# The rows that stand apart: W_q times (W_k transposed times the rows), two heads at once, in place of the folded weights times the rows

## The chip, the cores and the metric

The kernel runs on one core of a Trainium2 chip. The metric is the device time of one execution in microseconds (us), the median of several runs; lower is better. Engines are named as in the profile: PE (TensorE matmuls), PEld (its weight loads), DVE (VectorE), ACT (ScalarE), POOL (GpSimd) and SP (the queue that issues nearly all DMAs). All arithmetic that matters here is float32, and one float32 matmul of the program stands as two records in the trace; a transpose on PE stands as one.

## The reference, cut to what matters

The model has two layers. Each begins with a cross attention in which 64 latent rows per batch element (16 batch elements, 128 numbers wide) attend, in 16 heads of 64, over the 1601 rows of a context and over themselves:

```
xn, ln_lat = layer_norm(x, g1, b1), layer_norm(latents, g2, b2)
q  = ln_lat @ Wq
kv = concatenate([xn, ln_lat], axis=1) @ Wkv
k, v = split(kv, 2, axis=-1)
weight = softmax(einsum('bhld,bhnd->bhln', q * scale, k * scale))     # scale**2 = 1/8
out = einsum('bhln,bhnd->bhld', weight, v)
return out.transpose(0, 2, 1, 3).reshape(b, l, heads * dim_head) @ Wout
```

After the attention come, in layer 0, a state-space scan and a mixture of experts, and in layer 1 another scan and a feed-forward part. They are woven between the attention's tiles and are not touched by the change.

## The kernel before

**Folded weights.** The score of a latent row with a context row in head h is ln_lat · (Wq_h Wk_hᵀ / 8) · xnᵀ. The kernel folds the two weights of each head into one 128x128 matrix once per layer (`fold_qk`, which runs `fold`, matmuls L344, evictions L349 and L351), kept in `wqk`. `queries` (L455) multiplies the latents by it, and `scores` (L662) multiplies the result with the context rows as they are. `fold_vo` folds the value and the output weights in the same way into `wvo` (tiles `WvT`, also L344).

**Tiling.** A group is one batch element and eight heads, so there are 64 groups. A group's scores are made in 13 tiles of 128 context rows by 512 columns (eight heads times 64 latents). 13 tiles hold 1600 context rows and the 64 latent rows. One context row of the 1601 is left over for each batch element: these 16 rows "stand apart".

**The rows that stand apart.** `apart(lay)` prepares them once per layer. It normalises the 16 rows (L370 to L382), writes them to DRAM (`xed`, L383), transposes them (`xet` L386, copied into `xeT`, 128x16), and then makes `ge`, which holds for each batch element and head the 128-vector (Wq_h Wk_hᵀ / 8) · row. Before the change it does so from `wqk`, four heads at a time and four times: PE transposes four 128x128 matrices into a PSUM tile (`wkq`, L394), ACT copies it to SBUF (`wkq0s`, L396), PE multiplies each by `xeT` (L399, 16 columns), and DVE copies the result into `ge` (L400). `apart_scores` (L409, L414) later multiplies the latents of two batch elements by `ge`; `maximum` needs its result.

**What sets the order.** The program is recorded in steps `n`, one per score tile. In each step the loop in `run` resumes the generators whose turn has come (`yield HOP3` asks to be resumed three steps later, a plain number only ends the step's share), and `behind` ties what they emit to the last score tile of each engine, so that each engine executes in an order fixed beforehand. DMAs issued from SP are placed more freely. All engines execute their own list strictly in order: an instruction that waits holds up all behind it on its engine.

**Buffers that the change touches.** `tp` gives PSUM tiles from a pool of three banks, shared by the transposes, `kt`, `q`, `WqT`, `WvT`, `wkq`, `ge`, `se` and others; a new tile waits until an older one in its bank has been read. The score tiles have three banks of their own. In SBUF the tag `raw` has three buffers of 2 KB per partition: they hold `xw`, the four `wkq0s`, and the raw weights of layer 1. The tag `st2` has twelve buffers: the scores of a group take six, and the raw weights of layer 0 (`raw0`, loaded first of all) use four of them until they are given back.

**Who stands behind `apart(0)`.** While it runs, the kernel is still filling its pipeline. On DVE the statistics of the second batch element's context (L594, L595) lie between its instructions; they end in `crstd` (L598). POOL then takes its power of minus one half (L135), makes `coff` (L600, L601), ACT normalises eight tiles with it (L606), SP stores the normalised context (`xh`, L632), and behind that store on SP stand the loads of the raw weights for `fold_vo(0)`.

Of the kernel before, what the change touches and what calls it, by code (L numbers as in the profile page):

```python
# [32 lines left out]
F32 = mybir.dt.float32  # L33
# [9 lines left out]
P = 128  # L43
NB, L, D = 16, 64, 128
# [6 lines left out]
H, DH = 16, 64  # L51
# [13 lines left out]
HOP1, HOP, HOP3, HOP4 = (1,), (2,), (3,), (4,)  # L65
# [14 lines left out]
class Kernel:  # L80
# [273 lines left out]
    def fold_qk(self, lay):  # L354
        self.wqk = self.at.tile([P, H, D], F32, tag="wqk", name=f"wqk{lay}")
        yield from self.fold(lay, self.wqk, "WqT", "WkT", 0.125)
        self.raw0 = None

    def fold_vo(self, lay):
        self.wvo = self.at.tile([P, H, D], F32, tag="wvo", name=f"wvo{lay}")  # L360
# [1 line left out]
    def apart(self, lay):  # L362

        nc = self.nc
        w1 = self.vecs_of(lay)[0]
        xe = self.xe
        if lay == 0:
            mean, rstd, v = (self.sm([NB, 1], f"e{x}") for x in ("mean", "rstd", "var"))
            scr = self.at.tile([NB, D], F32, tag="raw", name="escr", bufs=3)
            nc.vector.tensor_reduce(mean, xe, AX.X, ALU.add)  # L370
            nc.vector.tensor_scalar_mul(mean, mean, 1.0 / D)
            nc.vector.tensor_scalar(xe, xe, mean, None, ALU.subtract)
            nc.scalar.activation(scr, xe, AF.Square)
            yield HOP1
            nc.vector.tensor_reduce(v, scr, AX.X, ALU.add)
            nc.vector.tensor_scalar(v, v, 1.0 / D, 1e-5, ALU.mult, ALU.add)
            nc.gpsimd.tensor_tensor(rstd, v, self.neghalf[:NB, :1], ALU.pow)
            yield HOP1
            nc.vector.tensor_scalar(xe, xe, rstd, None, ALU.mult)
        xw = self.at.tile([NB, D + 1], F32, tag="raw", name=f"xw{lay}", bufs=3)  # L380
        nc.vector.memset(xw[:, D:], 1.0)
        nc.vector.tensor_tensor(xw[:, :D], xe, self.vec[:NB, w1, :], ALU.mult)  # L382
        nc.sync.dma_start(out=self.xed[lay], in_=xw)  # L383
        yield HOP
        t = self.tp(f"xet{lay}")
        nc.tensor.transpose(t[:, :NB], xw[:, :D], self.ident[:NB, :NB])  # L386
        self.xeT = self.at.tile([P, NB], F32, tag="xeT", name=f"xeT{lay}")
        nc.vector.tensor_copy(self.xeT, t[:, :NB])
        yield 0.7
        self.ge = self.at.tile([P, NB, H], F32, tag="ge", name=f"ge{lay}")  # L390
        for g in range(H // 4):
            t = self.tp(f"wkq{lay}_{g}")
            for k in range(4):
                nc.tensor.transpose(t[:, k * D:(k + 1) * D], self.wqk[:, g * 4 + k, :], self.ident)  # L394
            w = self.at.tile([P, 4, D], F32, tag="raw", name=f"wkq{lay}s{g}", bufs=3)
            nc.scalar.copy(w.rearrange("p h d -> p (h d)"), t)  # L396
            o = self.tp(f"ge{lay}_{g}")
            for k in range(4):
                nc.tensor.matmul(o[:, k * NB:(k + 1) * NB], w[:, k, :], self.xeT, start=True, stop=True)  # L399
            nc.vector.tensor_copy(self.ge[:, :, g * 4:g * 4 + 4], o[:, :4 * NB].rearrange("p (h b) -> p b h", h=4))  # L400
            yield 0.7

    def apart_scores(self, lay, c):


        nc = self.nc
        xnT = self.lat_of[lay, c // CG][0][:, (c % CG) * P:(c % CG + 1) * P]
        t = self.tp(f"se{lay}_{c}")
        nc.tensor.matmul(t[:, :2 * H], xnT, self.ge[:, 2 * c:2 * c + 2, :].rearrange("p b h -> p (b h)"), start=True, stop=True)  # L409
        for j in range(2):  # L410
            se = self.sm([P, H // 2], "se")
            mine = t[j * L:(j + 1) * L, j * H:(j + 1) * H].rearrange("p (n i) -> p i n", i=2)
            for i in range(2):
                nc.vector.tensor_copy(se[i * L:(i + 1) * L, :], mine[:, i])  # L414
            if lay:
                nc.vector.tensor_scalar(se, se, self.mex[:, 2 * c + j:2 * c + j + 1], None, ALU.add)
            self.se_of[lay, 2 * c + j] = se
        yield 0.6
# [1260 lines left out]
```

## Time and profile before

| what | value |
|---|---|
| median of 3 runs | 1976.11 us |
| lowest, highest | 1975.02, 1976.44 us |
| the profiled execution, its own time | 1976.84 us |
| its span in the trace, first to last instruction | 1975.1 us |
| PE busy | 1931.2 us, 98% of the span |
| DVE busy | 1584.3 us, 80% |
| ACT busy | 1385.2 us, 70% |
| POOL busy | 510.4 us, 26% |
| granted PE clock | 0.999 |

The profiled execution took 0.73 us longer than the median; 1.7 us of its time lie outside the span. "Busy" counts the union of an engine's instructions, so matmuls that overlap are counted once. A row of the profile names a line of the kernel, the engine, the operation and the tiles written and read; in a timeline the columns are start, length, engine, line and operation, and in brackets the idle time before it and what ended it.

### The profile page before, as it was taken

How to read it: one execution, taken by the hardware profiler on the slowest of the kernel's cores; microseconds unless marked ns; L12 is line 12 of the kernel's file. 1: busy time of each engine (PE TensorE's matmuls, PEld its weight loads, DVE VectorE, ACT ScalarE, POOL GpSimd, SP SyncE). 2: the span in 40 equal slices, each digit the busy share in tenths (PEclk: the TensorE clock that was granted, in tenths of full speed). 3: DMA queues.
4: the chain of work that ended last, by engine and by line, in shares of the span. 5: the costliest groups of instructions: out<-in, count | busy, mean ns of one | idle time of the engine just before them, and what ended most of it. 6: DMA issues, size and time to landing. Idle time of an engine off the chain costs nothing. (4 is left out here: it accounts for less than half of the span.)

```text
span 1975.1 us, 32602 instructions
## 1 busy us (share of the span) xinstructions
PE 1931.2 (98%) x11971; PEld 1478.7 (75%) x11971; DVE 1584.3 (80%) x3025; ACT 1385.2 (70%) x2642; POOL 510.4 (26%) x579
## 2 busy tenths in 40 slices
PE   8999999999999999999999999999999999999998
PEld 5777777677777767778777777777778777787786
DVE  6977776987878887876998878898786978778875
ACT  5888787887868888666776657776665665766651
POOL 5111122543123452121452203442110111101000
PEclk9999999999999999999999999999999999999999
DMA  6121112312123221221221112221120210101000
GB/s 184 49 71 47 36 54 81 85 62 70 45 66 86 76 66 53 66 79 45 69 82 54 41 35 67 71 58 54 48 68 1 58 37 20 58 18 37 23 1 22
DMA packets 144109, 110.80 MB, mean 56 GB/s; under 512 B 13762, under 2 KB 130254, under 8 KB 143950
## 3 DMA queue, kind: packets, MB, share of 16 engines
q1 hardware_dynamic: 143406, 108.46, 18.8%
q8 instruction: 95, 1.56, 0.3%
q14 instruction: 64, 0.52, 0.1%
q10 hardware_dynamic: 544, 0.26, 0.0%
HBM read 80.23 MB, written 27.41 MB: 54 GB/s over the span
## 5 line engine op out<-in xcount | busy, mean ns | idle before, releaser
L725 PEld LDWEIGHTS av<-kv,st 128*128 128x128 f32 x6656 | 870.0, 192 | 375.7 <-issue 356.3
L725 PE MATMUL av<-kv,st 128*128 128x129 f32 x6656 | 882.2, 275 | 4.1 <-DVE aq L734 4.0
L662 PE MATMUL s<-qT,kvT 128*128 128x512 f32 x1664 | 857.7, 598 | 9.1 <-ACT st L677 6.6
L713 ACT ACTIVATE st<-st 128x1024 f32<-128x1024 f32 (+1 forms) x448 | 444.4, 996 | 121.6 <-DVE st L712 114.8
L712 DVE TENSOR_TENSOR st<-st,mb 128x1024 f32<-128x1024 f32 (+1 forms) x448 | 503.5, 1134 | 17.9 <-PE mb L704 17.8
L675 ACT ACTIVATE st<-s,mcol 128x512 f32<-128x512 f32 x416 | 283.4, 684 | 191.4 <-DVE R L670 167.2
L677 ACT COPY st<-s 128x512 f32<-128x512 f32 x416 | 240.0, 580 | 127.7 <-DVE R L672 117.2
L670 DVE SCALAR_TENSOR_TENSOR R<-s,mcol,R 128x512 f32<-128x512 f32 x352 | 261.9, 744 | 44.0 <-PE s L662 42.8
L672 DVE TENSOR_TENSOR R<-s,R 128x512 f32<-128x512 f32 x352 | 240.7, 684 | 64.0 <-PE s L662 62.6
L662 PEld LDWEIGHTS s<-qT,kvT 128*128 128x128 f32 x1664 | 254.4, 191 | 24.7 <-ACT st L677 11.5
L578 POOL TENSOR_TENSOR kv<-kv,vec 128x384 f32<-128x384 f32 (+1 forms) x128 | 130.8, 1042 | 146.9 <-PE kt L637 35.2
L774 POOL TENSOR_TENSOR aq<-aq,rd 128x512 f32<-128x512 f32 x63 | 74.4, 1181 | 340.8 <-DVE rd L773 329.3
L878 POOL TENSOR_TENSOR db<-sc_u,bb 128x512 f32<-128x512 f32 x64 | 83.6, 1309 | 123.5 <-DVE h L889 63.9
L895 POOL TENSOR_TENSOR sc_y<-sc_y,h 128x512 f32<-128x512 f32 x60 | 80.9, 1349 | 117.4 <-DVE h L894 100.9
L889 DVE TENSOR_TENSOR_SCAN h<-da,db 128x512 f32<-128x512 f32 x64 | 91.4, 1429 | 0.5 <-ACT da L877 0.5
L628 ACT ACTIVATE kv<-kv,coff,crstd 128x128 f32<-128x128 f32 x182 | 76.2, 490 | 6.0 <-POOL coff L625 6.0
L734 DVE SCALAR_TENSOR_TENSOR aq<-xeb,ee,av 128x129 f32<-128x129 f32 x252 | 76.2, 341 | 0.0
L619 ACT ACTIVATE scr<-kv,cmean 128x128 f32<-128x128 f32 x182 | 72.6, 399 | 2.8 <-DVE cmean L615 0.6
L135 POOL TENSOR_TENSOR crstd<-cvar,neghalf 128x13 f32<-128x13 f32 x14 | 34.2, 2440 | 138.5 <-DVE cvar L623 138.1
L455 PE MATMUL q<-xnT,wqk 128*128 128x128 f32 x512 | 68.4, 277 | 0.0
L455 PEld LDWEIGHTS q<-xnT,wqk 128*128 128x128 f32 x512 | 62.6, 192 | 2.9 <-issue 1.4
L672 DVE TENSOR_TENSOR R<-s,st 128x512 f32<-128x512 f32 x32 | 22.0, 687 | 52.0 <-PE s L662 43.4
(412 smaller groups left out, 1939.1 us busy)
## 6 DMA issues: line engine op xcount, KB each, us to landing
bb<-bcd SPq DMA_DIRECT2D x64, 256.0 KB, 4.5
xh<-kv SPq DMA_DIRECT2D x16, 832.0 KB, 4.7
kv<-xh SPq DMA_DIRECT2D x16, 832.0 KB, 5.5
kvT<-xhT SPq DMA_DIRECT2D x16, 800.0 KB, 4.6
xhT<-kvT SPq DMA_DIRECT2D x15, 800.0 KB, 3.4
kv<-in_ctx_dram SPq DMA_DIRECT2D x15, 768.0 KB, 5.4
ew<-in_e1T_dram SPq DMA_DIRECT2D x36, 64.0 KB, 1.8
ew<-in_e3T_dram SPq DMA_DIRECT2D x36, 64.0 KB, 2.0
```

Of the source, the lines that this page charges most:

```text
L455: nc.tensor.matmul(t[:, k * P:(k + 1) * P], self.wqk[:, g * 4 + k, :], xnT, start=True, stop=True)
L578: nc.gpsimd.tensor_tensor(kv[:, lo:hi, :D], kv[:, lo:hi, :D], self.row(self.vec[:, w1, :], [P, hi - lo, D]), ALU.mult)
L662: mm = nc.tensor.matmul(s, self.kv_of[lay, b][1][:, i * P:(i + 1) * P], q, start=True, stop=True)
L670: mx = nc.vector.scalar_tensor_tensor(R, s, mc, last, ALU.add, ALU.max)
L672: mx = nc.vector.tensor_tensor(R, s, last, ALU.max)
L675: ev = nc.scalar.activation(st, s, AF.Identity, bias=mc)
L677: ev = nc.scalar.copy(st, s)
L712: nc.vector.tensor_tensor(st, st, self.row(mb, [P, n, NQ]), ALU.subtract)
L713: nc.scalar.activation(st, st, AF.Exp)
L725: nc.tensor.matmul(grp["av", j][:, k, :], st, self.kv_of[lay, b][0][:, i, :], start=(i == 0 and k == 0), stop=(i == NT - 1 and k == 1))
L878: nc.gpsimd.tensor_tensor(db, u, self.row(bb[:, 0, s % 2, :], both), ALU.mult)
L889: nc.vector.tensor_tensor_scan(flat(h), flat(da), flat(db), 0.0, ALU.mult, ALU.add)
```

## The change

`ge` is made by another product: Wq_h · (Wk_hᵀ · row), scaled by 1/8 in between, from the raw weights. The raw weights hold two heads of 64 in 128 partitions, so that one 128x128 block of W_k stands for two heads.

- A new inner function `turned(n)` (n is 0 or 1) transposes four blocks of W_k (tile `wk`, eight heads) and copies them to SBUF with ACT. In layer 0 the raw weights are those still held in `raw0`; in layer 1 `turned` loads them again with two DMAs of 256 KB (`gWqT`, `gWkT`), and goes on three steps later.
- For each n, four matmuls multiply them by `xeT` (tile `kx`, 128x16 each, two heads at once); DVE scales the result by 0.125 into SBUF.
- Eight matmuls with 64 rows each (two heads per block, alternating between the upper and the lower half of the partitions) multiply W_q by it into two PSUM tiles, and DVE copies each into its half of `ge`.
- `raw0` is given back at the end of `apart` instead of at the end of `fold_qk`. In layer 0 the two calls of `turned` stand before the transpose of the rows, which comes later by one hop.

```
     def fold_qk(self, lay):
         self.wqk = self.at.tile([P, H, D], F32, tag="wqk", name=f"wqk{lay}")
         yield from self.fold(lay, self.wqk, "WqT", "WkT", 0.125)
-        self.raw0 = None
...
     def apart(self, lay):
         nc = self.nc
+        def turned(n):
+            if lay == 0:
+                raw = [[self.raw0[2 * n + m // 2][x][:, m % 2, :] for m in range(4)] for x in range(2)]
+            else:
+                raw = []
+                for x in ("WqT", "WkT"):
+                    t = self.at.tile([P, 4, D], F32, tag="raw", name=f"g{x}{n}", bufs=3)
+                    nc.sync.dma_start(out=t, in_=self.a[f"L1{x}"].rearrange("(m p) d -> p m d", p=P)[:, 4 * n:4 * n + 4, :])
+                    raw.append([t[:, m, :] for m in range(4)])
+                yield HOP3
+            t = self.tp(f"wk{lay}{n}")
+            for m in range(4):
+                nc.tensor.transpose(t[:, m * P:(m + 1) * P], raw[1][m], self.ident)
+            w = self.at.tile([P, 4, D], F32, tag="raw", name=f"wk{lay}s{n}", bufs=3)
+            nc.scalar.copy(w.rearrange("p m j -> p (m j)"), t)
+            wk.append((w, raw[0]))
+            yield 0.7
+        wk = []
...
         nc.sync.dma_start(out=self.xed[lay], in_=xw)
-        yield HOP
+        if lay:
+            yield HOP
+        else:
+            for n in range(2):
+                yield from turned(n)
+            yield HOP1
         t = self.tp(f"xet{lay}")
...
         self.ge = self.at.tile([P, NB, H], F32, tag="ge", name=f"ge{lay}")
-        for g in range(H // 4):
-            t = self.tp(f"wkq{lay}_{g}")
-            for k in range(4):
-                nc.tensor.transpose(t[:, k * D:(k + 1) * D], self.wqk[:, g * 4 + k, :], self.ident)
-            w = self.at.tile([P, 4, D], F32, tag="raw", name=f"wkq{lay}s{g}", bufs=3)
-            nc.scalar.copy(w.rearrange("p h d -> p (h d)"), t)
-            o = self.tp(f"ge{lay}_{g}")
-            for k in range(4):
-                nc.tensor.matmul(o[:, k * NB:(k + 1) * NB], w[:, k, :], self.xeT, start=True, stop=True)
-            nc.vector.tensor_copy(self.ge[:, :, g * 4:g * 4 + 4], o[:, :4 * NB].rearrange("p (h b) -> p b h", h=4))
+        for n in range(2):
+            if lay:
+                yield from turned(n)
+            w, wq = wk[n]
+            t = self.tp(f"kx{lay}{n}")
+            for m in range(4):
+                nc.tensor.matmul(t[:, m * NB:(m + 1) * NB], w[:, m, :], self.xeT, start=True, stop=True)
+            kx = self.sm([P, 4, NB], "kx")
+            nc.vector.tensor_scalar_mul(kx.rearrange("p m b -> p (m b)"), t[:, :4 * NB], 0.125)
+            yield 0.5
+            ts = [self.tp(f"ge{lay}{n}{i}") for i in range(2)]
+            for m in range(4):
+                for i in range(2):
+                    half = slice(i * DH, (i + 1) * DH)
+                    nc.tensor.matmul(ts[i][:, m * NB:(m + 1) * NB], wq[m][half], kx[half, m, :], start=True, stop=True)
+            for i in range(2):
+                to = self.ge[:, :, 8 * n:8 * n + 8].rearrange("p b (m i) -> p i b m", i=2)[:, i]
+                nc.vector.tensor_copy(to, ts[i][:, :4 * NB].rearrange("p (m b) -> p b m", m=4))
             yield 0.7
+        self.raw0 = None
```

## The prediction

> **What bounds the kernel now.** I read the page's busy shares and costliest groups first, then the tiles of `apart` one by one, then the timeline from 0 to 50 us (PE, ACT, DVE, POOL, SP) and from 900 to 990 us, and the waits of PE there. The page:
>
> ```profile
> PE 1931.2 (98%) x11971; PEld 1478.7 (75%) x11971; DVE 1584.3 (80%) x3025; ACT 1385.2 (70%) x2642; POOL 510.4 (26%) x579
> L725 PE MATMUL av<-kv,st 128*128 128x129 f32 x6656 | 882.2, 275 | 4.1 <-DVE aq L734 4.0
> L662 PE MATMUL s<-qT,kvT 128*128 128x512 f32 x1664 | 857.7, 598 | 9.1 <-ACT st L677 6.6
> ```
>
> PE is the bound: it idles some 44 us of 1975, and its two big groups wait for almost nothing. So only two things can move the time: PE work, where PE never waits, and the few places where it does. The tiles that the change removes, and the nearest relative of what it adds:
>
> ```profile
> L394 PE MATMUL wkq<-ident,wqk x32: 272/273/328, 22.9 to 924.4; 128*128 128x128 f32 x32
> L396 ACT COPY wkq0s<-wkq x4: 585/586/616, 23.5 to 32.5; 128x512 f32<-128x512 f32 x4
> L399 PE MATMUL ge<-xeT,wkq0s x32: 179/263/263, 24.2 to 34.6; 128*128 128x16 f32 x32
> L344 PEld LDWEIGHTS WqT<-rawWqT x32: 182/186/188, 6.1 to 14.5; 64*128 64x128 f32 x32
> L344 PE MATMUL WqT<-rawWqT x32: 272/272/373, 6.1 to 14.6; 64*128 64x128 f32 x32
> ```
>
> A record's length (273 ns) is not its price, because records overlap. The price is the distance to the next start, from the timeline of PE:
>
> ```profile
> 12.25 0.71 PE L344 MATMUL WqT<-rawWqT 64*128 64x128 f32 x8
> 12.90 1.12 PE L662 MATMUL s<-qT,kvT 128*128 128x512 f32 x2
> 22.89 0.60 PE L394 MATMUL wkq<-ident,wqk 128*128 128x128 f32 x4
> 23.33 1.02 PE L662 MATMUL s<-qT,kvT 128*128 128x512 f32 x2
> 24.19 1.04 PE L399 MATMUL ge<-xeT,wkq0s 128*128 128x16 f32 x8
> 25.09 1.14 PE L455 MATMUL q<-xnT,wqk 128*128 128x128 f32 x8
> ```
>
> Four transposes cost 0.44 us (0.11 a record), eight 128-row records of 16 columns 0.90 (0.11), eight 64-row records on alternating halves 0.65 (0.081). A score tile costs 0.86.
>
> Then the start of layer 0, the chain that decides here (POOL, ACT, SP, PE):
>
> ```profile
> 32.98 2.46 POOL L135 TENSOR_TENSOR crstd<-crstd,neghalf 128x13 f32<-128x13 f32 x1 [0.98 <-DVE crstd L598]
> 36.80 0.88 ACT L606 ACTIVATE kv<-kv,coff,crstd 128x128 f32<-128x128 f32 x2 [3.25 <-POOL coff L601]
> 41.49 0.57 SPq L632 DMA_DIRECT2D xh<-kv  x1
> 43.27 1.29 SPq L326 DMA_DIRECT2D rawWvT<-in_L0Wo_dram  x1
> 47.61 0.57 PE L344 MATMUL WvT<-rawWvT 64*128 64x128 f32 x3 [0.74 <-DMA rawWvT<-in_L0Wo_dram]
> ```
>
> DVE's `crstd` L598 releases POOL, POOL's `coff` releases ACT, the last of ACT's eight L606 (ended 41.43) releases the `xh` store, and behind it on SP stand the third pair of raw value weights, for which PE waits 0.74 us. From 48 to 100 us PE has no gap but one of 0.37: what arrives at 47.61 arrives at the end. Layer 1, waits of PE from 900 to 1000 us and the busy times of a stretch:
>
> ```profile
> PE s L662 <- ACT st L675: 1.0, 2, 0.8
> PE mb L704 <- DVE m L693: 0.5, 1, 0.5
> 932.00:962.00 30.00, 29.49 (x178) 22.00 (x177) 27.87 (x46) 20.82 (x35) 13.95 (x12) 1.00 0.31 78
> ```
>
> From 912 to 932 PE is busy 20.00 of 20 us and DVE 8.74; from 932 to 985 DVE is at 51 of 53, and PE's 1.5 us of waits follow DVE's score maxima.
>
> **PE work, per layer.** Removed: 16 transposes, 4 x 0.44 = 1.76, and 16 matmuls (32 records), 4 x 0.90 = 3.60; together 5.36. Added: 8 transposes 0.88, 8 `kx` matmuls (16 records of the same shape as L399) 1.80, and 16 matmuls of 64 rows and 16 columns (32 records). No row shows these. The nearest, `WqT`, has the same weights and the same alternation of halves, with 128 columns: 32 x 0.081 = 2.6. Below it: if two halves ran wholly side by side, 0.055, 1.8. Above: The Trainium skill, "TensorE: Matmul & The Clock Gate", section "LDWEIGHTS (loading the stationary operand)", says that a weight load costs its columns over 1.2 GHz and not its rows, so a 64-row load would take the full 107 ns: 32 x 0.107 = 3.4. This rule speaks against the change. The length of the load agrees (186 ns against 191 at 128 rows); the distance between starts does not (0.081 against 0.11), so I take the row, 2.6. Sum: 5.28 for 5.36, -0.08; by the rule +0.7; at the lower end -0.9. Halving the transposes thus buys almost nothing: the second product pays it back.
>
> **ACT and DVE, per layer.** ACT loses two of four copies of 586 ns, about 1.0 us. DVE keeps four copies of 225 ns and gains two scalings of about 0.17 (`xeT`'s copy took 0.17). ACT is 70% busy, so its saving lies beside PE. If that cover went, 1 us would show.
>
> **Layer 0, walked along the recorded order.** `wk0` and `wk1` (0.44 each) fall behind the second `kt` and the next score tile, at 16.2 and 17.6, where PE idled about 1.4 us between 17 and 20.5: free. The fourth score tile's maximum still comes at 20.35 on DVE (behind the 1.34 us wait for POOL's `erstd`), and ACT, in order, empties it at 21.6 and then the third quarter of the queries at 22.2; only then has `q` its bank. So: `q` 22.3, score 23.2, `kx0` 24.1, score, `kt`, score until 26.9 (DVE scales at 25.8), `ge0` 1.3 to 28.2, score 29.0, `kx1` 29.9 (its bank waits for DVE's `xt`, 27.3), score 30.8, `ge1` until 32.1, three scores; the first of the next group waits for ACT until 34.1 and ends at 35.0 instead of 35.9. That 0.9 us isn't kept:
>
> - The first `WvT` waits for its load. On SP the first raw weights of layer 1 now stand ahead of it and wait for `xet`, `kx0` and `kx1` (21, 25, 30 us); but the `kv` store behind them waits for POOL until 32.0 anyway, as before. The load is issued 0.2 earlier, 33.5 for 33.69, so PE starts at about 36.3 for 36.48.
> - DVE's `crstd` now stands behind the copy of the first half of `ge1`: 32.1 plus 0.2 (PE to DVE) plus 0.2 makes 32.5, plus 0.15 gives 32.65 for 32.9. POOL is free at 32.0. So `coff` comes 0.3 earlier, 36.45, and PE's second tile of the next group about 0.7 earlier.
> - ACT then interleaves differently: one more score copy stands ahead of the last L606. Eight L606 and four score copies from 36.45 make 8 x 0.40 + 4 x 0.47 = 5.1, so 41.6 for 41.43 (eight and three made 4.6). `xh` and the loads behind it move by +0.15, and PE's wait grows from 0.74 to over 1.
>
> Layer 0: +0.15. If `ge` were at 0.107 a record, `crstd` comes 0.8 later and this is +0.95; at 0.055, POOL's 32.0 is the floor and it is -0.4.
>
> **Layer 1.** `wk10`, `kx10` and `ge10` stand between 919 and 931, but `wk11`, `kx11` and `ge11` (0.44 + 0.90 + 1.3 = 2.6) move behind the fifth to seventh score tile of the next group, into 932 to 948. PE's total by then is the same, so up to there it runs 2.6 ahead and DVE, which sat idle 5.67 us before 932.39, starts its full stretch 2.6 sooner. It carries 0.6 more in it (a scaling and two copies) and waits about 0.4 for `kx11`: counted from the fourth score tile's end, PE has `kx11` after 6.2 us, DVE asks after 6.0, plus the hop; for `ge11` PE needs 9.3 and DVE asks at 9.5. Queued behind these DVE waits are the scan step, the subtraction and the maxima, for which ACT and PE wait. A lead of about 1.5 remains, which could cover all 1.5 us of PE's waits; since DVE stays full to 1010, part comes back as a later wait. I take half, -0.7; both ends 0 and -1.5.
>
> DMAs: `gWqT0` goes at about 893, `gWkT0` at 902, the second pair when `wk10` and `kx10` are done; 256 KB rows land in 2.8 to 4.5 us and PE asks for `wk11` about 12 us after `kx10`. Behind them on SP the value weights slip from 919 to about 945 (needed at 1016), and the scan's rows went at 948 before: covered by 3 us there, and if not, one wait of that size.
>
> **Sum.** +0.15 - 0.08 - 0.7 = about -0.6: 1976.84 to 1976.2 for the profiled execution, and 1976.11 to 1975.5 for the median, which stands 0.73 lower. What can be told from no change here is about 0.2%, 3.95 us.
>
> **Rivals.** (1) No visible change, by the sum: 1975.5, chance 0.62; its own range is 1974 to 1977.
>
> (2) Slower, the hops in front of `crstd`: `apart(0)` is now a chain PE, DVE, PE, DVE, and DVE's in-order `crstd` waits for its end. Each us by which `ge1` ends after about 32.2 goes 1:1 through POOL, ACT and `xh` to PE at 47.6. With the rule's full loads (+0.8 there, +0.7 on PE in layer 1), no relief in layer 1 and 0.6 of extra hops: 0.15 + 0.8 + 0.7 + 0.6 = 2.3, 1978.4. It decides from 0.09 us a record. For: `crstd` has no slack. Against: the `WqT` row. 0.20, with a tail of 0.09 beyond 1980.1, where the stores and loads of the start also collide.
>
> (3) Faster: cheap 64-row records (-0.9 in layer 1, -0.4 at the start) and all waits of layer 1 gone, -1.5: about 1973.3. For: 16 columns are fewer than `WqT`'s 128. Against: 128-row records cost 0.11 with 16 columns as with 128. 0.18, with 0.08 beyond 1972.2, where later waits of PE (44 us in all) would also have to shrink.
>
> That the change doesn't do what it says is excluded: the program holds 8 transposes per layer for 16.
>
> **Numbers.** Predicted 1975.5. The range, 1973.0 to 1978.9, takes in the ends of the unknown costs in both rivals and leaves out about 0.18. Faster by over 0.2% 0.08, within 0.83, slower 0.09.
>
> **What would show it.** Right: `ge` records 0.08 apart; `xh` of the second element within 0.3 of 41.6 and PE still waiting for `rawWvT` at about 47.8; PE's 1.5 us of waits near 962 to 972 smaller; ACT busy down 2 us with the span unmoved. Wrong: 0.11 a record; `crstd` after 33.5; a PE wait on `gWkT` or `kx`; or PE idle in 932 to 960 for `av`, behind DVE's `aq`.

## The result, and the profile after

The changed kernel takes 1973.3 us (median of 22 runs, 1971.66 to 1977.24) against 1976.45 us (22 runs, 1975.02 to 1979.06): ratio 0.9984, interval 0.9978 to 0.9990, about -3.1 us. The prediction was -0.6, range 1973.0 to 1978.9. The size of the gain was wrong by a factor of five; where it comes from, still more so.

The page after: the span is 1971.6 us (before 1975.1), the profiled execution's own time 1973.36 us (before 1976.84).

```profile
PE 1931.2 (98%) x11987; PEld 1478.8 (75%) x11987; DVE 1582.9 (80%) x3029; ACT 1383.5 (70%) x2638; POOL 512.3 (26%) x579
L760 PE MATMUL av<-kv,st 128*128 128x129 f32 x6656 | 881.8, 275 | 4.0 <-DVE aq L769 4.0
L697 PE MATMUL s<-qT,kvT 128*128 128x512 f32 x1664 | 859.3, 599 | 7.4 <-ACT st L712 5.5
```

PE's busy time is the same to the tenth, with 16 more records, and ACT lost 1.7 us. So the 3.5 us are idle time of PE, it seems. That reading deceives, because busy time counts a record at half clock as longer. The new tiles:

```profile
L378 PE MATMUL wk<-ident,rawWqT x8: 272/272/273, 16.3 to 18.0; 128*128 128x128 f32 x8
L380 ACT COPY wk1s<-wk x2: 586/588/589, 919.3 to 937.0; 128x512 f32<-128x512 f32 x2
L422 PE MATMUL kx<-xeT,wk0s x16: 179/263/263, 24.1 to 29.8; 128*128 128x16 f32 x16
L431 PEld LDWEIGHTS ge<-kx,rawWqT x32: 182/188/188, 27.2 to 31.8; 64*128 64x128 f32 x32
L431 PE MATMUL ge<-kx,rawWqT x32: 259/259/280, 27.2 to 31.8; 64*128 64x16 f32 x32
```

Their starts, with the waits at the start of layer 0 (timeline of PE, then POOL, ACT, SP):

```profile
24.07 0.96 PE L422 MATMUL kx<-xeT,wk0s 128*128 128x16 f32 x8
27.17 1.07 PE L431 MATMUL ge<-kx,rawWqT 64*128 64x16 f32 x16
28.17 1.12 PE L697 MATMUL s<-qT,kvT 128*128 128x512 f32 x2
36.77 1.14 PE L344 MATMUL WvT<-rawWvT 64*128 64x128 f32 x8 [1.82 <-DMA rawWvT<-in_L0Wo_dram]
48.37 0.68 PE L344 MATMUL WvT<-rawWvT 64*128 64x128 f32 x4 [0.65 <-DMA rawWvT<-in_L0Wo_dram]
32.46 2.46 POOL L135 TENSOR_TENSOR crstd<-crstd,neghalf 128x13 f32<-128x13 f32 x1 [0.47 <-DVE crstd L633]
36.28 0.49 ACT L641 ACTIVATE kv<-kv,coff,crstd 128x128 f32<-128x128 f32 x1 [2.51 <-POOL coff L636]
41.65 0.50 ACT L641 ACTIVATE kv<-kv,coff,crstd 128x128 f32<-128x128 f32 x1
42.21 0.57 SPq L667 DMA_DIRECT2D xh<-kv  x1
```

Sixteen `ge` records take 28.17 - 27.17 = 1.00 us, 0.0625 each. The eight `WvT` records at 36.77 took 1.14 us where they took 0.71 before: PE's clock was at half. Busy times from 37 to 41 us, the granted clock in the third column from the right:

```profile
37.00:41.00 4.00, 4.00 (x17) 2.49 (x16) 1.87 (x7) 3.53 (x9) 2.36 (x4) 0.59 0.03 7
```

The trace's record of the clock has it at 0.5 for 3.41 us, from 36.9. Such stretches also come elsewhere, in some executions and not in others (one near 1607 to 1610 us in the profiles of before and after), at about 1.7 us each, half of 3.41; so below, places of the trace are compared rather than spans alone.

The profile's gain is laid out by taking one and the same PE instruction in both traces and subtracting its starts, after minus before:

| PE instruction at | after minus before | what lies in between |
|---|---|---|
| 50 us | +0.76 | start of layer 0, slow clock |
| 640 to 650 us | +0.88 to +0.58 | a wait of 0.45 at 643 down to 0.15 |
| 860 to 912 us | -1.16 | three waits that the change does not touch |
| just past 1012 us | -2.84 | layer 1 |
| 1900 us | -2.70 | both have a slow stretch near 1607 to 1610 |
| 1955 us | -2.99 | a wait of 0.24 at 1927 gone |

So layer 1 gave 1.7 us, and nearly 2 us came between 640 and 860 us (1.7 of it after 650), of which the prediction has no word. Layer 1's waits of PE from 900 to 1000 us, and the stretch that was shown of before:

```profile
PE kx L422 <- ACT wk1s L380: 0.6, 1, 0.6
PE s L697 <- ACT st L710: 0.2, 1, 0.2
```

```profile
932.00:962.00 30.00, 29.45 (x190) 22.41 (x189) 28.30 (x47) 19.36 (x35) 16.49 (x13) 1.00 0.32 93
```

The waits of 0.51 and 0.76 for DVE's maxima and ACT's `st` are gone; a new one, for ACT's copy of the transposed weights, takes 0.55 (rounded to 0.6 here). Now the middle, with the same lines of before first (DVE's mean of a loaded context, then ACT's shift after a store):

```profile
818.89 1.09 DVE L613 TENSOR_REDUCE cmean<-kv 128x7 f32<-128x896 f32 x1 [1.62 <-DMA kv<-in_ctx_dram]
739.00 1.82 ACT L646 ACTIVATE kvT<-kvT,vcol 128x768 f32<-128x768 f32 x2 [2.21 <-DMA xhT<-kvT]
```

and of after:

```profile
817.73 1.09 DVE L648 TENSOR_REDUCE cmean<-kv 128x7 f32<-128x896 f32 x1 [0.77 <-DMA kv<-in_ctx_dram]
738.68 1.81 ACT L681 ACTIVATE kvT<-kvT,vcol 128x768 f32<-128x768 f32 x2 [1.88 <-DMA xhT<-kvT]
```

Both are waits for a transfer, 700 us after anything that the change did to layer 0, and PE stands behind them. Its waits of before at 741 us for `st` and at 838 us for `sg` (the first two lines) are gone after (the last two):

```profile
741.34 1.12 PE L662 MATMUL s<-qT,kvT 128*128 128x512 f32 x2 [0.37 <-ACT st L677]
838.26 0.71 PE L1022 MATMUL me<-ew,sg 128*128 128x128 f32 x4 [0.68 <-DVE sg L1045]
741.01 1.13 PE L697 MATMUL s<-qT,kvT 128*128 128x512 f32 x2
837.11 0.70 PE L1057 MATMUL me<-ew,sg 128*128 128x128 f32 x4
```

The third of the three waits in the table is one for DVE's `tm` at 703 us, 1.42 us before and 0.80 after. Over all the profiles of this document it varies from 0.80 to 1.47 us, with the old layer 0 (1.01 to 1.42) as with the new, so that its 0.6 us belongs to this one execution. What is left for the change to explain is the 1.2 us from 740 us on (+0.02 to -1.16).

### The profile page after: what moved, and what is told of

It reads as the page before. It is cut to its first block, busy times and chain, and to the rows that moved or that the text cites. A ratio compares the mean times of both kernels' runs of the same rounds, so it can differ in the third digit from the quotient of the medians.

```text
span 1971.6 us, 32642 instructions
## 1 busy us (share of the span) xinstructions
PE 1931.2 (98%) x11987; PEld 1478.8 (75%) x11987; DVE 1582.9 (80%) x3029; ACT 1383.5 (70%) x2638; POOL 512.3 (26%) x579
## 5 line engine op out<-in xcount | busy, mean ns | idle before, releaser
L681 ACT ACTIVATE kvT<-kvT,vcol 128x768 f32<-128x768 f32 (+1 forms) x62 | 58.2, 959 | 3.9 <-DMA xhT<-kvT 3.9
```

## The experiments

Ratios are to the kernel before, on the same chip, with the 95% interval.

### One layer at a time

Both forms of `apart` in one kernel, chosen by the layer:

```diff
+    def apart(self, lay):
+        return self.apart_new(lay) if lay == 0 else self.apart_old(lay)     # second kernel: lay == 1
```

> Layer 0 has the new way, layer 1 the way of before. Theory A (the gain is layer 1's, and the start only loses, by the slowed PE clock after a longer wait for the first value weights; what was gained between 640 and 860 us was the luck of one execution): 0 to +1 us against before, PE at 48 us late by about 0.8. Theory B (the gain between 640 and 860 us belongs to the change of layer 0 and returns in each execution): -1 to -1.5 us, with the same shift back between 640 and 860 us. In both the waits near 962 to 972 us stay at 1.5 us.

Measured: 1975.09 against 1977.01 us, ratio 0.9990 (0.9984 to 0.9997). PE at 50 us is 0.56 late, with the slow clock and the wait of 1.82 us again. Then the same PE instructions come back from +0.96 at 650 us to -0.73 at 850: 1.7 us, as in the changed kernel (1.4 of it after 740 us). Waits near 961 to 972 us: 0.50, 0.77, 0.22, as before. The execution in the profile had the same span as before (1975.1) because it lost 1.0 us of that again between 1150 and 1350 us; the runs say -2. So Theory A, which had 0 to +1 us and no return of the shift, is wrong.

> Layer 1 has the new way, layer 0 the way of before. Theory A: -1.7 us against before (cheap records 0.8, waits 0.9), most of what the whole change gave; no loss at the start. Theory B: -1.7 us as well, but then the whole change's -3.1 needs layer 0's share too, and layer 0 alone must show it. If the gain between 640 and 860 us shows here, where nothing ahead of 890 us is changed, it belongs to neither layer.

Measured: 1974.3 us, ratio 0.9984 (0.9976 to 0.9993). In the profile PE is at +0.06 at 650 us, +0.01 at 850, -1.64 at 1012. So layer 1 alone is worth 1.65 us in the trace, and with the old layer 0 there is no gain between 650 and 860 us: Theory B stands, by one profile of each kernel. The intervals of the two ratios are too wide to add them up to the whole.

### The price of a 64-row record

```diff
-            for m in range(4):
-                for i in range(2):
+            for i in range(2):
+                for m in range(4):
                     half = slice(i * DH, (i + 1) * DH)
```

> The changed kernel with the 16 products of ge in the order of four of one half, then four of the other, for alternating halves. If the alternation makes the 64-row record cheap: 0.11 us from start to start for 0.0625, PE work +1.5 us per layer, the time +1.5 to +3 us against the changed kernel (about -1.5 to 0 against before). If few rows or 16 columns alone make it cheap: 0.0625 still, and the time of the changed kernel.

```profile
27.17 1.53 PE L431 MATMUL ge<-kx,rawWqT 64*128 64x16 f32 x16
28.64 1.12 PE L697 MATMUL s<-qT,kvT 128*128 128x512 f32 x2
```

Sixteen records take 1.47 us, 0.092 each, for 0.0625 in the other order: the same loads and the same matmuls, 0.9 us more per layer. The load's own length is the same (188 ns median in both). So the order makes a third of the record's price, and both orders are under the 0.10 to 0.11 of a 128-row record: neither of the two expected prices came. In layer 1 PE is 1.0 us later than in the changed kernel by 1012 us, as the records' price has it. Time 1975.17 us, ratio 0.9988 (0.9982 to 0.9995), an interval that overlaps that of the changed kernel. One rival is open: where the half of the partitions alternates, the PSUM tile that is written alternates with it, in this edit too, and no run parts the two.

### The lead of DVE in layer 1, with no cheaper work

The kernel before, with two quarters of the old `ge` put later:

```diff
-            yield 0.7
+            yield (8,) if lay and g == 1 else 0.7
```

> The kernel before, with the third and fourth quarter of layer 1's ge (2.7 us of PE) put behind the fifth and sixth score tile of the next group; no work is changed. If the lead that DVE gets by this takes PE's waits away: PE's 1.5 us of waits near 962 to 972 us go to 0.2 to 0.8, the time -0.7 to -1.3 us. If the gain of layer 1 is only the cheaper products: no change, waits as before or a new one for the copies on ACT.

PE's waits from 900 to 1000 us:

```profile
PE ge L399 <- ACT wkq1s L396: 0.6, 1, 0.6
PE s L662 <- ACT st L675: 0.2, 1, 0.2
```

This is the picture of after, the new wait for ACT's copy included. From 900 to 1012 us PE gains 1.4 us (+0.52 to -0.90) with not one operation changed. By the runs the ratio is 0.9994 (0.9988 to 1.0001), so the time alone could not have told. In the traces, moving the work is thus worth about as much as the change in layer 1. The effect of POOL on DVE that the last section describes has a small part in it at most: the two operations concerned took 0.70 and 1.00 us here, for 1.07 and 1.00 before.

### PE's instruction loads and the context transfers

What of layer 0 could act 700 us later? The order of work there is back to that of before by 100 us. What stays is that PE's stream is longer by 8 loads and 8 matmuls. The trace has packets of kind "instruction" on one queue, 95 in all of 16 KB, which by their number fit PE's stream of 24,000 loads and matmuls (one per 252; the Trainium skill, "Advanced Engine Details and Errata", section "ISA Cache", has 16 KB for 256 instructions). Near the load of a context at 812 to 818 us one comes at 815.9 us in the profile of before, at 816.0 and 816.1 in the two experiments with the old layer 0, but at 813.0, 813.2 and 812.9 in the three with the new one. In the load itself it makes this difference: with the old layer 0 the packet starts 2.7 to 3.0 us after the load was issued, while its data moves, and the load lands 6.0 to 6.1 us after its issue; with the new one the packet starts 0.3 to 0.6 us after the issue, ahead of the data, and the load lands after 5.3 to 5.5 us. So 8 transposes that nobody reads were put into the kernel before:

```diff
         t = self.tp(f"xet{lay}")
+        if lay == 0:
+            for _ in range(8):
+                nc.tensor.transpose(t[:, P:2 * P], self.ident, self.ident)
```

> The kernel before with 8 transposes of the identity that nobody reads, ahead of the transpose of xet in layer 0, where PE sits idle 1.2 us; no other instruction is added or moved. They make PE's instruction stream as much longer by there as the new layer 0 does (8 weight loads and 8 matmuls). Theory B1 (the gain between 640 and 860 us comes from where PE's instruction loads fall against the context transfers): ACT's wait at 739 us goes from 2.2 to about 1.5, DVE's at 819 from 1.6 to about 0.9, PE's start at 860 us comes 1.2 to 1.6 earlier against its start at 640, and the time is -1 to -1.5 us. Theory B2 (the order of the transfers or the work of the other engines in layer 0 does it): waits and time as before, within 0.2.

Measured: 1974.05 against 1976.24 us, ratio 0.9989 (0.9980 to 0.9998). DVE's wait at 819 us is 0.62, ACT's at 739 is 1.80; PE gains 1.3 us between 650 and 850 (-1.46 to -2.79). But it also gained 1.18 us at the start, which the expectation had not: the pads changed the order on DVE, `crstd` ran ahead of the `ge` copies, at 30.7 us for 32.7, and its result came down the chain of the prediction:

```profile
31.81 2.45 POOL L135 TENSOR_TENSOR crstd<-crstd,neghalf 128x13 f32<-128x13 f32 x1
40.31 0.57 SPq L635 DMA_DIRECT2D xh<-kv  x1
46.43 0.68 PE L344 MATMUL WvT<-rawWvT 64*128 64x128 f32 x4 [0.55 <-DMA rawWvT<-in_L0Wo_dram]
```

POOL starts 1.17 earlier than before, `xh` 1.18, PE 1.18: one to one, as predicted for that chain. To keep the start as it was, the pads were put elsewhere:

```diff
-        t = self.tp(f"at{g}")
+        t = self.tp(f"at{g}"); [nc.tensor.transpose(t[:, :P], self.ident, self.ident) for _ in range(8 * (g == 10))]
```

> The kernel before with 8 transposes of the identity that are written over unread, ahead of the turn of the heads' sums near 368 us, where PE waits 0.67 us; the order of all engines up to there is that of before. They make PE's instruction stream 8 loads and 8 matmuls longer from there on, as the new layer 0 does from 32 us on. If the place of PE's instruction loads against the context transfers makes the gain: the 16 KB packet near 816 us starts about 3 us sooner in the program, DVE's wait at 819 us goes from 1.6 to 0.6 to 1.0 and ACT's at 739 from 2.2 to about 1.6, PE gains 1 to 1.5 us between 640 and 860 us, and the pads cost 0 to 0.3 near 368. If the order of work in layer 0's start makes it: both waits as before and +0.2 us.

```profile
819.88 1.09 DVE L613 TENSOR_REDUCE cmean<-kv 128x7 f32<-128x896 f32 x1 [1.11 <-DMA kv<-in_ctx_dram]
740.51 1.82 ACT L646 ACTIVATE kvT<-kvT,vcol 128x768 f32<-128x768 f32 x2 [1.45 <-DMA xhT<-kvT]
839.24 0.71 PE L1022 MATMUL me<-ew,sg 128*128 128x128 f32 x4 [0.16 <-DVE sg L1045]
```

With nothing changed ahead of 368 us, PE gains 1.36 us between 650 and 860 (+2.34 to +0.98), and the packet comes at 814.8 us, 0.4 us after the load's issue for 2.95 and 2.6 us sooner in the program than before (PE stood at +1.5 there). The profile's +1.9 at 50 us is a slow stretch of the clock at 39 us and a longer wait behind it, both ahead of the edit. By the runs 1974.77 against 1976.79 us, ratio 0.9993 (0.9984 to 1.0002). Over all profiles with the old layer 0 and no pads (before and two more) the DVE wait is 1.50 to 1.62 us and the ACT wait 2.21 to 2.45; over the nine with the longer stream, 0.62 to 1.11 and 1.10 to 1.88. The load takes 6.0 to 6.1 us in the three and 5.1 to 5.6 in the nine, and from 740 to 850 us PE shifts by 0.05 and 0.10 us in the other two of the three and by -1.0 to -2.0 in the nine, whether it came early (-1.4, the pads in layer 0) or late (+2.3, the pads at 368 us). That a stream longer by this much brings the gain is thus shown in the traces; by the run times alone, the kernel with the pads at 368 us can't be told from the kernel before. That it does so by a collision of the packet with the load fits its place in all twelve profiles, and was not tried by itself; neither were other numbers of pads.

### The slow clock at 37 us

Two matmuls of 512 columns that nobody reads, ahead of the first `WvT`, to cover PE's 1.82 us:

```diff
             ts = [self.tp(f"{l}{lay}{g}{i}") for i in range(2)]
+            if (lay, l, g) == (0, "WvT", 0):
+                for _ in range(2):
+                    nc.tensor.matmul(ts[0], self.ident, self.wqk[:, :4, :].rearrange("p h d -> p (h d)"), start=True, stop=True)
```

> The changed kernel with two matmuls of 512 columns whose result nobody reads (1.7 us), ahead of the first value weights' product in layer 0, where PE sat idle 1.82 us and its clock then fell to half for 3.4 us. If the idle time brings the slow clock: no slow stretch at 37 to 40 us, PE at 50 us 0.7 to 0.9 earlier than in the changed kernel, and the time -0.5 to -0.8 against it. If the slow stretch comes by chance of the run: it shows as often, and the time is the same.

```profile
32.89 1.88 PE L343 MATMUL WvT<-wqk,ident 128*128 128x512 f32 x4
36.44 0.72 PE L347 MATMUL WvT<-rawWvT 64*128 64x128 f32 x8 [1.66 <-DMA rawWvT<-in_L0Wo_dram]
```

Busy times of the same execution from 37 to 41 us, the granted clock (1.00) third from the right:

```profile
37.00:41.00 4.00, 4.00 (x18) 2.05 (x14) 2.75 (x9) 3.04 (x8) 2.31 (x3) 1.00 0.05 15
```

They ran ahead of the score tiles and did not fill the gap, which stayed 1.66 us; yet the clock stayed full, and PE at 50 us came 0.22 us earlier than in the changed kernel, for an expected 0.7 to 0.9. The time is 1973.45 us, ratio 0.9985 (0.9976 to 0.9994): no gain in the runs. So the expectation is not settled.

What the traces' record of the clock does show is where such a stretch can start. In all twelve profiles every stretch at half clock starts a whole number of 3.413 us after the clock first became full, and that first moment differs from execution to execution (4.8 to 7.6 us into the span). PE waits 1.2 to 1.8 us in one piece near 1605 to 1610 us in every profile. Where one interval of this 3.413 us grid held 1.6 us or more of that idle time, the next one ran at half clock (six profiles, 1.61 to 1.84); where the grid split the wait (five profiles) or the wait was short (one), no interval held more than 1.46 us, and the clock stayed full. Near 37 us the same count gives 1.20 to 1.82 us of idle time in the interval just ahead of the seven slow stretches, and 0.21 to 1.09 in four of the five profiles without one; this run, with 1.66, is the exception. The idle time alone is not the whole rule: near 1415 us the kernel before had an interval with 1.81 us of it, and the clock stayed full.

### The new wait in layer 1, and the chain of layer 0

`kx` and `ge` of layer 1's second half one score tile later:

```diff
             wk.append((w, raw[0]))
-            yield 0.7
+            yield HOP if lay and n else 0.7
```

> The changed kernel with kx and ge of layer 1's second half one score tile later. The new wait of PE for ACT's copy of the transposed weights (0.55 us at 938 us) goes. If it is on the path: -0.3 to -0.55 us against the changed kernel. If DVE, full from 930 to 1010 us, is the bound there: the same time, with a wait of that size for the score tiles or for mb later.

```profile
PE s L697 <- ACT st L710: 0.2, 1, 0.2
```

That is all that PE waits for from 900 to 1000 us. Against the changed kernel it gains 0.95 us between 912 and 1012 (-0.19 to -1.13), more than the wait of 0.55: start to start, the wait had cost 0.81, and one of 0.18 at 1010 us fell to 0.04. Time 1971.49 against 1976.24 us, ratio 0.9978 (0.9969 to 0.9987).

The third pair of value weights asked for with the second:

```diff
-            else:
-                raw = self.raw_pair(lay, l, r, g, nc.sync)
+            elif (lay, l) == (0, "WvT"):
+                for k in {1: (1, 2), 2: ()}.get(g, (g,)):
+                    pre[k] = self.raw_pair(lay, l, r, k, nc.sync)
+                raw = pre[g]
```

> The changed kernel with the third pair of raw value weights of layer 0 asked for together with the second, ahead of the xh store on SP's queue. If the chain of the prediction holds (crstd, POOL, ACT, xh, load, PE): PE's wait of 0.65 us for the third pair at 48 us goes, and the time is -0.4 to -0.65 against the changed kernel. If other waits stand right behind it: the same time, and PE waits for kvT or st there.

Measured: 1971.88 us, ratio 0.9978 (0.9969 to 0.9987). PE's wait at 48 us is gone and PE at 50 us is 0.52 earlier than in the changed kernel, as expected. In layer 1, however, the profile loses 0.9 us against the changed kernel (+0.03 at 912 to +0.95 at 985 us, of which 0.2 comes back at 1010), with a wait of 0.73 for `st`:

```profile
951.45 4.33 POOL L617 TENSOR_TENSOR kv<-kv,vec 128x512 f32<-128x512 f32 x4 [0.60 <-DMA kv<-xh]
951.70 0.96 DVE L455 TENSOR_SCALAR se<-se,mex 128x8 f32<-128x8 f32 x1
966.86 1.12 PE L701 MATMUL s<-qT,kvT 128*128 128x512 f32 x2 [0.73 <-ACT st L714]
```

Both together:

> The changed kernel with both: the third pair of raw value weights of layer 0 asked for ahead of the xh store, and kx and ge of layer 1's second half one score tile later. The two lie 890 us apart; if each keeps its gain, PE's waits at 48 us and at 938 us are both gone and the time is 0.8 to 1.4 us under the changed kernel, about 1971 to 1972. If DVE gives back a wait near 967 us, as it did with the earlier load alone, it is 0.7 more.

1972.92 against 1976.79 us, ratio 0.9980 (0.9971 to 0.9989). Both waits are gone in the profile (PE's first `WvT` of the third pair at 47.91 us waits for nothing, no `kx` wait at 938), and the wait near 967 us, 0.63, is back here too: the second case of the expectation. The version with `kx` later alone is as good as any; it, the earlier load and both of them lie within each other's intervals, and all three intervals overlap that of the changed kernel (0.9978 to 0.9990), so that no gain of theirs over it is shown by the runs.

## Why the prediction was right and wrong

It held in its verdict, no change over 0.2%, and in its range, by 0.3 us at its lower end. The likeliest time was off by 2.2 us, and the terms of the sum by more, since errors of both signs met; that the range held is in good part luck. Of the signs that it named for being right, the smaller waits near 962 to 972 us and the 1.7 us less of ACT came; the records were at 0.0625 and not 0.08, `xh` left 0.6 us late, and the span did move.

- **The price of `ge`.** I took 0.081 us a record, from `WqT`, for a range of 0.055 to 0.107. It is 0.0625: 32 records make 2.0 for 2.6 us, so PE's work per layer is -0.7, not -0.08. The full 107 ns a record, whatever the rows, is refuted for this stream: the length of a load is the same (188 ns) and the price is not (0.0625 in alternating order, 0.092 in the other). The same page of the Trainium skill ("TensorE: Matmul & The Clock Gate", section "Part 3: Packing small matmuls — row/col tiling") says that loads run beside matmuls in flight only where the row groups differ; the experiment with the other order fits that, and it should have been weighed against the first.
- **Layer 0, `wk` in idle time, POOL and `crstd`.** `wk` fell at 16.3 and 17.6 us as walked, `crstd` ended at 32.38 for a forecast 32.65, the first L641 started at 36.28 for 36.45. Right.
- **Layer 0, the first load.** Forecast 0.2 earlier, found level (33.72 us for 33.69) and 2.9 us to land, so PE started at 36.77 for 36.48. The walk itself has PE idle from 35.0 to 36.3 us there. The step that failed is that this idle time has no price beyond its length: 1.82 us of it was followed by half a clock for 3.41 us. In that stretch PE's score tile at 38.28 took 2.05 us for 1.1, DVE's maximum at 40.45 came later, the score copy ahead of ACT's last L641 waited 0.65 us for it, and `xh` left at 42.21 for a forecast of 41.6. PE was at +0.76, not +0.15. ACT's own work was walked rightly: from its first L641 to the end of the eighth it takes 5.87 us here, and 5.11 for the forecast 5.1 in the run with the other order of `ge`, where the clock stayed full. The Trainium skill's page, section "What's actually happening", describes such a step down after an idle window of about 3.4 us that runs free of the program. The 3.41 us and the grid that is free of the program are in these traces; a window that was idle throughout is not, 1.20 to 1.82 us of idle time stood in it.
- **Layer 1, the lead of DVE.** I took half of 1.5 us. PE's three waits and the one at 1012 us fell from 1.82 to 0.95 us with the new 0.55 in it: -0.87 for -0.7. The move alone does as much. Start to start, a wait costs more than the idle time that the profile gives it: the two of 0.51 and 0.76 that went brought 0.67 and 0.98, and the new one of 0.55 cost 0.81. With 0.15 from the wait at 1012 and 0.7 from the cheaper records this makes up the 1.7 us. The wait on `kx`, which I named as a sign that would make me wrong, came; I had set ACT's copy at nothing there, though ACT's copy stands behind `st` copies that wait for DVE. It was covered by the larger rest, and moving `kx` one tile on took it away.
- **What was missing.** About 1.2 us from 740 us on, 1.0 to 2.0 in all profiles that have a longer PE stream. I counted instructions only by their time. Rival (3) gave 1973.3 by cheap records and the end of all waits: its number is the measured one by luck, for its reasons make half of it, in layer 1, while the start lost where it had a gain.

## What to carry to other kernels

Place the gain before explaining it: subtract the starts of the same instructions in both traces, and look at every stretch where the difference moves, also where nothing was changed. Look at the same place in several profiles before you call a difference the change's: one wait here moved by 0.6 us on its own. A change in the length of an engine's instruction stream can move its instruction loads against later transfers, as 8 loads and 8 matmuls did here; a control with as many empty instructions, put where they are covered, tells this from the work itself. Let products on halves of 64 rows alternate, as here (0.0625 for 0.092 us). When the copy that a product needs stands in a full queue, putting the product one slot later takes its wait away.

## What the runs showed of the hardware that was not expected

- 64-row products of 16 columns cost 0.0625 us each on alternating halves (and PSUM tiles), 0.092 with four in a row on the same half, 0.10 to 0.11 with 128 rows.
- Eight empty transposes at 368 us brought PE 1.36 us between 650 and 860 us, with DVE's and ACT's waits for two transfers down by 0.5 and 0.8.
- PE's clock fell to half only at whole multiples of 3.413 us from its first full moment (all 25 stretches of the twelve profiles). One and the same wait near 1607 us brought it where one such interval held 1.61 us or more of idle time, and did not where none held over 1.46.
- DVE's small operation `se<-se,mex` (128x8) takes 0.22 us, but when POOL is running as it starts, it ends only as POOL's instruction does: in all 27 such cases of before and after together, 0.02 to 0.06 us after the end of one, with lengths from 0.22 to 1.21 us. In the kernel before, both that follow the start of POOL's `kv<-kv,vec` pay:

```profile
951.68 3.01 POOL L578 TENSOR_TENSOR kv<-kv,vec 128x512 f32<-128x512 f32 x3
951.82 1.06 DVE L416 TENSOR_SCALAR se<-se,mex 128x8 f32<-128x8 f32 x1
953.71 1.00 DVE L416 TENSOR_SCALAR se<-se,mex 128x8 f32<-128x8 f32 x1
```

After, DVE is 2 us further on and the second one starts just ahead of POOL:

```profile
951.66 0.22 DVE L451 TENSOR_SCALAR se<-se,mex 128x8 f32<-128x8 f32 x1
951.71 4.36 POOL L613 TENSOR_TENSOR kv<-kv,vec 128x512 f32<-128x512 f32 x4 [0.90 <-DMA kv<-xh]
```

The 0.78 us that this saves DVE is about the wait of 0.76 that PE lost near 968 us. With the earlier load of the third pair POOL started 0.26 sooner, the second one took 0.96 again, and PE's wait was back at 0.73. So a part of what I put down to the lead in layer 1 can be this; it was read from the traces and not tried by itself. It isn't needed for it: where the work was only moved, the second one took 1.00 us and PE's wait of 0.76 was gone all the same. The Trainium skill, "SBUF — State Buffer", section "SBUF: two separate sides", says that of a GpSimd operation and certain kinds of DVE operation the one that starts first holds their shared ports for its whole instruction, and the other is blocked. The rows agree with that, if this operation is of such a kind.
